# When routing makes its list: ahead of the scatters in attention 0, with weights asked for early and row copies one per step

## The chip, the cores and the metric

The kernel runs on one core of a Trainium2 chip. The metric is the device time of one execution in microseconds (us), given as a median over several runs. TensorE (PE) multiplies, VectorE (DVE) and ScalarE (ACT) work on tiles element by element, GpSimd (POOL) issues the indirect transfers, and SyncE (SP) issues the other transfers between the chip's memory (HBM) and the tiles.

## What is computed

The reference is two layers on x of 4 batches x 512 tokens x 256, all in fp32:

```python
x = x + L0_xattn(layernorm(x), ctx)      # 8 heads of 4
x = x + L0_ffn(layernorm(x))             # 8 experts, top 2, at most 640 tokens each
x = x + L1_xattn(layernorm(x), ctx)      # 16 heads of 16
x = x + L1_ffn(layernorm(x))             # 15 experts, top 3, and one shared expert
```

A token's expert in layer 0 is found from softmax logits, its place among that expert's tokens by counting in token order, and tokens beyond the capacity of 640 are dropped:

```python
probs = softmax(clip(xn @ Wr.T)); top_p, top_i = top_k(probs, 2)
rank  = position of the token among those that chose the same expert
buf[expert, rank] = xn[token]            # rank < 640
h = silu(buf @ Wg.T) * (buf @ Wu.T); y = h @ W3.T
out[token] += top_p * y[expert, rank]
```

## The kernel before

**Stages.** Attention 0, the experts of layer 0, attention 1, the experts of layer 1. The expert stages work on tiles of tokens of one expert. Which expert a tile has is known only at run time, so a list of tiles is made on the chip, and SyncE reads the numbers out of it with value loads (`fetch0`, L958) to address rows (`rows0`, from the table `slots` in HBM) and weights (`w12`, 2 MB, and `w3`, 1 MB, for one expert).

**Attention.** `attention` (L561) is written as a software pipeline over steps t, whose order on TensorE, VectorE and ScalarE is set by hand. A step does two score matmuls with their row maximum (`maximum`, L695 and L700), two transposed score matmuls with the exponential (`exponential`, L719 and L724), and in every second step the product with the values (`weigh`, L734). A planner places the rest (projections, transposes L708, outputs L791) into steps by cost and due time. LEAD is 11: the maxima run eleven steps ahead of the exponentials.

**Routing beside it.** When a batch's attention is done, a generator starts for it (`behind0` in layer 0, `behind1` in layer 1), which calls `route` (L242): layer norm, copies of the normed rows into the rows to be scattered by ScalarE (L250, four per batch), eight PE transposes (L267), logits (L279), top-k, the running counts `past` (L319 to 322), softmax weights (L326 to 331), the place of each token (L352 to 369), and then, per group of 128 tokens (four) and choice (two), a scatter of rows into `slots` by GpSimd (L380). The generator yields between steps: V and PEP (a piece of VectorE or TensorE work, which costs credit), ACT (a piece of ScalarE work), or LITTLE (a step that costs nothing). Each attention step advances each generator by up to two items (L903 to 921). `pause` says that a generator does no more in this step:

```python
pause = w[1] == LITTLE and not shared
```

`shared` is true in attention 0, so there it never pauses. `w[2]` is the batch. `early` means batches 0 and 1 in attention 0; `hurry` that all attention steps are over (t > 8 * N) or have not begun.

**The list.** `listing` (L404) makes the list from the counts: a matmul of `past` (L419), some fifteen small VectorE operations (L422 to 455), and a matmul that moves the list onto one partition (L460). Its PSUM tile, `bank`, is one buffer which routing's transposes, logits, ranks and lists and attention 0's projections share.

**Early pairs.** After batch 1's routing, three pairs of full tiles (AHEAD = 3) can already be worked on. So behind batch 1's `route`, `behind0` makes a first list (`ahead0`), fetches the rows of the three pairs and asks for the weights of the first two. The rows wait for all scatters issued so far (`ffn0.puts`). Once attention 0's steps are over, `some_pairs` (L1036) runs these pairs: `turn0` (transposes, L980), `hidden0` (L998, eight pieces of four matmuls of 128x256), and `output0` (L1016, with a result scatter by GpSimd at L1022). Between its pieces the routing of batches 2 and 3 goes on. Behind batch 3's `route` a second list (`list0`) is made, and `pipeline` (L468, called at L1121) runs the remaining tiles: it fetches a tile's rows and W12 two tiles ahead, its W3 one ahead. All these transfers are issued by SyncE, in program order, on one queue.

**Attention 1.** It has 768-element row copies (three choices), and `some_shared` (L1255) puts pieces of the shared expert into the steps once its own steps are over.

Of the kernel before, what the change touches and what calls it, by code (L numbers as in the profile page):

```python
# [23 lines left out]
B, S, D = 4, 512, 256  # L24
# [25 lines left out]
TILES0 = -(-CAP // P)  # L50
# [4 lines left out]
AHEAD = 3  # L55
FULL0 = [(i + 1) * PAIR - 1 for i in range(CAP // PAIR)]
MOST0 = T * K0 // P + E0 - 1
# [18 lines left out]
def decoder_kernel(ctx: ExitStack, tc: tile.TileContext, a: dict, out: bass.AP):  # L76
# [6 lines left out]
    def after(ins, earlier, reason):  # L83
        for e in earlier:
            tc.add_manual_dep(
                ins, e.name,
                mybir.DependencyInfo(mybir.DependencyClass.Sync, mybir.DependencyReason.DATA),
                reason=reason,
            )
# [53 lines left out]
    early = ExitStack()  # L143
# [39 lines left out]
    V, ACT, PEP, LITTLE = "VectorE", "ScalarE", "TensorE", "little"  # L183
# [55 lines left out]

            self.expert, self.slot, self.token, self.base = expert, slot, token, base  # L240

    def route(f, b, pool, bank):  # L242

        n, K, first = f.n, f.k, f is ffn0
        rows = []
# [74 lines left out]
        for k in range(TB):  # L320
            nc.vector.tensor_tensor(past[:, k + 1, :], past[:, k, :], picked[:, k, :], ALU.add)
        f.past[b] = past

        yield V
        total = small.tile([P, TB], F32, name="sm_sum", tag="sm_sum")
# [42 lines left out]
        at = small.tile([P, TB, K], F32, name="at", tag="at")  # L368
# [3 lines left out]


        for k in range(TB):
            for _ in range(2):
                yield LITTLE
            nc.gpsimd.tensor_copy(rows[k][:, :, D + 1], weight[:, k, :])  # L377
            nc.vector.tensor_copy(put[k], at[:, k, :])
            for j in range(K):
                ins = nc.gpsimd.indirect_dma_start(  # L380
                    out=f.rows,
                    out_offset=bass.IndirectOffsetOnAxis(ap=put[k][:, j : j + 1], axis=0),
                    in_=rows[k][:, j, :],
                    in_offset=None,
                ).ins
                after(ins, f.fills, "empty rows under the rows")
                group = "puts" if first else "puts1"
                tc.declare_no_dep(ins, group=group, reason="disjoint rows")
                tc.add_to_no_dep_group(group, ins)
                f.puts.append(ins)  # L390
# [170 lines left out]
    def attention(L, begin, behind, others=None):  # L561
# [6 lines left out]
        shared = L == 0  # L568
# [19 lines left out]
        for i in range(NV):  # L588
            v = ap.tile([P, TB, (H - 1) * VS + 32], F32, name=f"v{i}", bufs=1)
            nc.gpsimd.memset(v, 0.0 if shared else 1.0)  # L590
            if shared:
                r = v.rearrange("p t (h i) -> p (t h) i", i=64)
                for s in range(2):
                    at = s * (32 + VR) + HD
# [226 lines left out]
        for b in range(B):  # L821
            at = 8 * U * b - LEAD
            starts[at - (26 if shared else 34)] = [lambda b=b: normalize(b)]
            turned = [task(at - 14, at - 6, lambda b=b, c=c: turn(b, c)) for c in range(DC)]
            for g in range(G):
                at = 8 * (U * b + 2 * g) - LEAD
# [9 lines left out]
            at = 8 * U * b  # L836
# [39 lines left out]
        with tc.manual_schedule(engines={ENG.PE, ENG.DVE, ENG.Activation}):  # L876
            while t <= last or (others and (going or pieces)):

                for j2 in range(2):
                    n, i = divmod(t + LEAD, 8)  # L880
                    if 0 <= n < N:
                        maximum(units[n], i, j2)
                    n, i = divmod(t, 8)
                    if 0 <= n < N:
                        exponential(units[n], i, j2)
                n, i = divmod(t - 3, 8)
                if 0 <= n < N and i % 2 == 0:
                    u = units[n]
                    weigh(u, i // 2)
                    if i == 6 and (not shared or u[2] == 1):  # L890
                        rest[u] = divide(u)
                if t == 4 - LEAD:
                    warm(AF.Exp)
                free = t not in steps
                credit = min(credit + RATE[L], 2 * RATE[L])
                if not free:
                    steps[t][0]()
                    credit -= steps[t][1]
                for start in starts.get(t, []):
                    work = start()  # L900
                    going.append([work, next(work), None])

                for w in sorted(going, key=lambda w: w[2] is not None):  # L903

                    early = shared and w[2] in (0, 1)
                    hurry = t > 8 * N or t < -LEAD
                    for _ in range(MOST[w[2] if early else None] if shared else 2):
                        if w[1] == PEP:
                            if not free:
                                break  # L910
                            free = False
                        if w[1] in (V, PEP):
                            if credit < (DEBT if early else COST) and not hurry:
                                break
                            credit -= COST
                        pause = w[1] == LITTLE and not shared
                        w[1] = next(w[0], None)
                        if w[1] is None:
                            going.remove(w)
                        if w[1] is None or pause:  # L920
                            break
                if others and t == 8 * N + 2:
                    pieces = others(ps_sc, wp, ap)
                if pieces and next(pieces, V) is V:
                    pieces = None
                t += 1
# [15 lines left out]
    def rows_of(t):  # L942
        return [t[:, k] for k in range(TB)]

    ffn0 = Routing(
        E0, K0, wr0, slots, zeros, lambda b: rows_of(mr0.tile([P, TB, K0, ROW], F32, name="rows", tag="rows"))
    )
    ffn1 = Routing(E1, K1, gw, xs, zeros1, None)
    ahead0 = const.tile([1, 2 * AHEAD + 1], I32, name="ahead0")
    list0 = const.tile([1, 2 * MOST0 + 1], I32, name="list0")  # L950
# [7 lines left out]
    def fetch0(j):  # L958
        rows0[j] = mr.tile([P, 2, ROW], F32, name="rows0", tag="rows0")
        at, i, n = (ahead0, j, AHEAD) if j < AHEAD else (list0, j - AHEAD, MOST0)  # L960
        r = nc.sync.value_load(at[0:1, n + i : n + i + 1], min_val=0, max_val=E0 * TILES0)
        m = 2 if j < AHEAD else 1
        src = tiles0[bass.ds(r, m)].rearrange("s p d -> p s d")
        after(nc.sync.dma_start(rows0[j][:, :m], src).ins, ffn0.puts, "rows in the slots")
        experts0[j] = nc.sync.value_load(at[0:1, i : i + 1], min_val=0, max_val=E0 - 1)

    def fetch_w12(j):
        load_w0(w12, "w12", a["W12T"], j, experts0[j])

    def fetch_w3(j):  # L970
        load_w0(w3, "w3", a["W3T"], j, experts0[j])
# [99 lines left out]

    def behind0(b):
        ffn0.xT[b] = mr0.tile([P, DC, S], F32, name="xT0", tag="xT0", bufs=1)
        yield from route(ffn0, b, mr0, bank)
        if b == 1:
            yield from listing(ffn0, b, ml0, bank, TILES0, AHEAD, ffn0.full, ahead0, size=2)
            for j in range(AHEAD):
                fetch0(j)
                if j < 2:
                    fetch_w12(j)  # L1080
                    fetch_w3(j)
        if b == B - 1:
            yield from listing(
                ffn0, b, ml1, bank, TILES0, MOST0, ffn0.some, list0, ffn0.taken, AHEAD
            )

    ml1 = routing.enter_context(tc.tile_pool(name="m0m", bufs=1))
    attention(0, begin0, behind0, some_pairs)
# [2 lines left out]
    with ExitStack() as first:  # L1091
        ps_h = first.enter_context(tc.tile_pool(name="ps_h", bufs=2, space=PSUM))
        ps_y = first.enter_context(tc.tile_pool(name="ps_y", bufs=2, space=PSUM))
        ps_t = first.enter_context(tc.tile_pool(name="ps_t", bufs=2, space=PSUM))
        mw = first.enter_context(tc.tile_pool(name="m0w", bufs=2))
        w0p.append(first.enter_context(tc.tile_pool(name="w02", bufs=1)))
        new = dict(
            pt=lambda: ps_t.tile([P, DC, P], F32, name="prt", tag="prt"),
            pg=lambda: ps_h.tile([P, PAIR], F32, name="pg", tag="pg"),
            pu=lambda: ps_h.tile([P, PAIR], F32, name="pu", tag="pu"),  # L1100
            py=lambda: ps_y.tile([P, D], F32, name="py", tag="py"),
            rT=lambda: mw.tile([P, DC, P], F32, name="rT0", tag="rT0"),
            hT=lambda: mw.tile([P, NF // 2, PAIR], F32, name="hT", tag="hT"),
            sg=lambda: mw.tile([P, PAIR], F32, name="sg", tag="sg"),
            ysb=lambda: mw.tile([P, D], F32, name="ysb", tag="ysb", bufs=6),
            parts=NF // 2,
        )

        def fetch(j):
            fetch0(j)  # L1110
            fetch_w12(j)

        def hidden(j):
            for _ in hidden0(j, new):
                pass

        def output(j):
            for _ in output0(j, new):
                pass

        pipeline(  # L1121
            AHEAD, AHEAD + ALWAYS0, [AHEAD + h for h in THEN0],
            lambda: nc.values_load(list0[0:1, 2 * MOST0 :], min_val=0, max_val=MOST0) + AHEAD,
            fetch, lambda j: turn0(j, new), hidden, output, fetch_w3,
        )
# [378 lines left out]
```

## Time and profile before

| quantity | value |
|---|---|
| median of 3 runs | 1227.63 us (1227.49 to 1232.14) |
| the profiled execution | 1229.34 us |
| its span, first to last instruction | 1227.6 us |
| mean granted TensorE clock | 0.957 of full |
| TensorE busy | 1155.8 us (94%) |
| VectorE, ScalarE, GpSimd busy | 619.2, 460.0, 187.8 us |
| DMA | 204.74 MB, 167 GB/s over the span |
| attention 0's last value product (L734) ends | 202.4 us |
| early pairs, first hidden matmul to the last output | 213.7 to 295.2 us |

The page gives busy times per engine, the span in 40 slices (one digit each: tenths of the slice in which the engine was busy, or tenths of full clock that TensorE was granted), and groups of instructions by line. The timeline lists one engine's instructions with start and duration in us; the square brackets hold the idle time right before it and what ended it. A row of windows gives the busy time of each engine in a stretch (with the number of instructions), then the granted clock, the DMA engines' busy share, and the rate. PE busy in a stretch with a clock of 0.50 is busy at half speed.

### The profile page before, as it was taken

Reading aid. Unit: us, or ns where it says so; the run is one execution under the profiler, and the core shown is the slowest. Engines: PE = TensorE matmul, PEld = TensorE weight load, DVE = VectorE, ACT = ScalarE, POOL = GpSimd, SP = SyncE. Lnnn points to the kernel's source line nnn. Section 1 sums busy time; section 2 is a strip of 40 time slices with the busy share of each in tenths; the row PEclk is TensorE's granted clock in tenths of the full one; section 3 lists DMA queues with packets and bytes.
Section 4 is the critical chain, followed back from the end, with each engine's and each line's share of the span. In section 5 each row is a group of like instructions: output and inputs, shape, how many; then the busy total and the mean of one; then the engine's idle time right before and its main releaser. Section 6 shows DMA issues by size and latency. Waiting matters only on the chain.

```text
span 1227.6 us, 18270 instructions
## 1 busy us (share of the span) xinstructions
PE 1155.8 (94%) x6582; PEld 742.3 (60%) x6582; DVE 619.2 (50%) x1591; ACT 460.0 (37%) x877; POOL 187.8 (15%) x274
## 2 busy tenths in 40 slices
PE   6999995989999999999999999999999999999992
PEld 3334332778999999996333433433346558888862
DVE  7677763531112111115768778767625435444426
ACT  2455454422222222213365566565543102333320
POOL 2000202051000000002000000211212401333330
PEclk9899988999999999999799999999979989999996
DMA  8999205338778888853101000101100134777737
GB/s 319 406 404 403 80 1 210 125 112 315 286 271 321 332 308 308 318 218 105 35 1 36 1 1 1 40 14 40 40 18 35 52 109 137 222 233 222 223 119 252
DMA packets 64406, 204.74 MB, mean 167 GB/s; under 512 B 9502, under 2 KB 31922, under 8 KB 57392
## 3 DMA queue, kind: packets, MB, share of 16 engines
q1 hardware_dynamic: 56144, 182.93, 41.9%
q0 software_dynamic: 8160, 20.52, 4.5%
q8 instruction: 55, 0.90, 0.3%
q14 instruction: 47, 0.39, 0.1%
HBM read 138.57 MB, written 66.70 MB: 167 GB/s over the span
## 4 chain that ended last, share of the span: by engine, by line
PE 43%; DVE 5%; DMA 3%; issue 2%; ACT 1%; POOL 0%; SPq 0%; POOLq 0%; DVEq 0%; ACTq 0%
PE sc L695 9%; PE av L734 5%; PE pg L1292 4%; PE pv L1292 4%; PE shared L1173 3%; PE pyp L1346 3%; PE sct L719 2%; DVE negmax L700 2%; PE pp L672 2%; PE shared L1188 1%; DMA y<-ysb,rows 1%; DMA yr<-y 1%; PE po L791 1%; PE pa L644 1%; PE pa L672 1%
## 5 line engine op out<-in xcount | busy, mean ns | idle before, releaser
L700 DVE TENSOR_REDUCE negmax<-sc 128x1 f32<-128x512 f32 x384 | 245.1, 682 | 68.3 <-PE sct L719 61.7
L724 ACT ACTIVATE es<-sct 128x512 f32<-128x512 f32 x384 | 208.7, 595 | 167.7 <-PE sct L719 148.6
L695 PE MATMUL sc<-kT,qT 32*128 32x512 f32 x768 | 257.4, 663 | 7.4 <-DVE negmax L700 4.4
L719 PE MATMUL sct<-qa,kT 32*128 32x512 f32 x768 | 259.8, 661 | 1.7 <-DVE qa L710 1.7
L695 PEld LDWEIGHTS sc<-kT,qT 32*128 32x128 f32 x768 | 83.2, 189 | 106.5 <-DVE negmax L700 61.4
L1007 DVE TENSOR_TENSOR hT<-pu,sg 128x256 f32<-128x256 f32 x96 | 40.8, 425 | 136.6 <-PE pu L998 133.1
L734 PE MATMUL av<-es,v 128*32 128x512 f32 x768 | 109.0, 628 | 0.0
L998 PE MATMUL pg<-rT,w 128*128 128x128 f32 x768 | 101.8, 275 | 0.4 <-ACT ahead L1020 0.4
L998 PE MATMUL pu<-rT,w 128*128 128x128 f32 x768 | 101.4, 275 | 0.0
L719 PEld LDWEIGHTS sct<-qa,kT 32*128 32x128 f32 x768 | 80.3, 189 | 26.1 <-issue 15.5
L998 PEld LDWEIGHTS pg<-rT,w 128*128 128x128 f32 x768 | 93.6, 192 | 0.8 <-ACT ahead L1020 0.6
L998 PEld LDWEIGHTS pu<-rT,w 128*128 128x128 f32 x768 | 93.5, 192 | 0.0
L1016 PE MATMUL py<-w,hT 128*128 128x256 f32 x384 | 86.7, 379 | 0.0
L1353 POOL DMA_INDIRECT y<-ysb,rows x60 | 59.1, 985 | 154.0 <-ACT ysb L1351 142.7
L1016 PEld LDWEIGHTS py<-w,hT 128*128 128x128 f32 x384 | 71.2, 190 | 8.7
L1003 ACT ACTIVATE sg<-pg 128x256 f32<-128x256 f32 x96 | 36.9, 384 | 101.7 <-PE pg L998 100.7
L377 POOL COPY rows<-weight 128x2 f32<-128x2 f32 (+1 forms) x28 | 4.4, 210 | 458.0 <-DVE weight L340 262.4
L734 PEld LDWEIGHTS av<-es,v 128*32 128x32 f32 x768 | 16.2, 109 | 77.9 <-issue 70.8
L1292 PE MATMUL pg<-rTp,wp 128*128 128x256 f32 x240 | 61.8, 380 | 0.6 <-DVE rTp L1330 0.6
L1292 PE MATMUL pv<-rTp,wp 128*128 128x256 f32 x240 | 61.6, 379 | 0.0
L1022 POOL DMA_INDIRECT y<-ysb,rows x24 | 23.6, 984 | 237.0 <-ACT ysb L1020 234.5
L1159 DVE TENSOR_SCALAR aTp<-pv,wp 128x256 f32<-128x256 f32 x60 | 32.6, 544 | 51.5 <-PE pv L1292 50.4
(257 smaller groups left out, 1493.6 us busy)
## 6 DMA issues: line engine op xcount, KB each, us to landing
w<-in_W12T_dram SPq DMA_DIRECT2D x27, 2048.0 KB
xs<-empty SPq DMA_DIRECT2D x61, 516.0 KB
w<-in_W3T_dram SPq DMA_DIRECT2D x27, 1024.0 KB
wp<-in_w1p_dram SPq DMA_DIRECT2D x30, 515.0 KB
yr<-y SPq DMA_DIRECT2D x20, 512.0 KB
rows<-xs SPq DMA_DIRECT2D x30, 258.0 KB
wp<-in_fc2T_dram SPq DMA_DIRECT2D x30, 256.0 KB
slots<-empty SPq DMA_DIRECT2D x11, 516.0 KB
```

What stands on the lines that cost most here:

```text
L672: nc.tensor.matmul(pp, W["W" + n][:, c, g * P : (g + 1) * P], rhs[:, c, :], start=(c == 0), stop=(c == DC - 1),)
L695: nc.tensor.matmul(sc, q[u][32 * j : 32 * j + 32, qt * P : (qt + 1) * P], k[u][32 * j : 32 * j + 32, :], start=True, stop=True,)
L700: nc.vector.tensor_reduce(heads[:, qt, j, HELP[s] : HELP[s] + 1], sc, AX.X, ALU.max, negate=True)
L719: nc.tensor.matmul(sc, k[u][32 * j : 32 * j + 32, kt * P : (kt + 1) * P], qa[u][32 * j : 32 * j + 32, :], start=True, stop=True,)
L724: nc.scalar.activation(t, sc, AF.Exp, scale=p["scale"])
L734: nc.tensor.matmul(av[b, g][32 * j : 32 * j + 32, :], vs[b % NV][:, kt, h : h + 32], es[u, kt, j], start=(first and kt == 0), stop=(last a ...
L998: nc.tensor.matmul(ph[:, i * n : (i + 1) * n], w[:, c, col + i * P : col + (i + 1) * P], rT[:, c, :], start=(c == 0), stop=(c == DC - 1),)
L1003: nc.scalar.activation(sg, pg, AF.Silu)
L1007: nc.vector.tensor_tensor(h, pu, sg, ALU.mult)
L1016: nc.tensor.matmul(py, hT[f][:, i * P : (i + 1) * P], w[:, f, :], start=(f == 0), stop=(f == NF - 1))
L1292: nc.tensor.matmul(ph[:, :n], w1[:, c, col : col + P], rhs[:, c, :], start=(c == 0), stop=(c == DC - 1),)
L1353: ins = nc.gpsimd.indirect_dma_start(out=y1, out_offset=bass.IndirectOffsetOnAxis(ap=rows[:, i, D : D + 1].bitcast(I32), axis=0), in_=ysb[ ...
```

## The change

`route` gets a hook, `counted`, that it runs as soon as the counts are made, ahead of the weights, the places and the scatters. `behind0` uses it to make the lists there. For batch 1 it also reads the experts of the three pairs and asks for the weights of the first two at that point; the rows are still fetched behind the scatters. For this, `fetch0` is split: the expert's value load becomes `name0`. Batch 1's scatters get three LITTLE items per group of tokens where they had two. `pause` changes: in attention 0 the scatters of batches 0, 2 and 3 now take one LITTLE item per step, and ScalarE's row copies of batches 2 and 3 in attention 0 and of all batches in attention 1 go one per step until the steps are over.

```diff
-    def route(f, b, pool, bank):
+    def route(f, b, pool, bank, counted=lambda: iter(())):
...
         f.past[b] = past
+        yield from counted()
...
-            for _ in range(2):
+            for _ in range(3 if first and b == 1 else 2):
                 yield LITTLE
...
-                        pause = w[1] == LITTLE and not shared
+
+                        pause = (
+                            w[1] == LITTLE and not (shared and w[2] == 1)
+                            or w[1] == ACT and w[2] is not None and not hurry and not early
+                        )
...
         after(nc.sync.dma_start(rows0[j][:, :m], src).ins, ffn0.puts, "rows in the slots")
+
+    def name0(j):
+        at, i = (ahead0, j) if j < AHEAD else (list0, j - AHEAD)
         experts0[j] = nc.sync.value_load(at[0:1, i : i + 1], min_val=0, max_val=E0 - 1)
...
-        yield from route(ffn0, b, mr0, bank)
+
+        def counted():
+            if b == 1:
+                yield from listing(ffn0, b, ml0, bank, TILES0, AHEAD, ffn0.full, ahead0, size=2)
+                for j in range(AHEAD):
+                    name0(j)
+                for j in range(2):
+                    fetch_w12(j)
+                    fetch_w3(j)
+            if b == B - 1:
+                yield from listing(
+                    ffn0, b, ml1, bank, TILES0, MOST0, ffn0.some, list0, ffn0.taken, AHEAD
+                )
+
+        yield from route(ffn0, b, mr0, bank, counted)
         if b == 1:
-            yield from listing(ffn0, b, ml0, bank, TILES0, AHEAD, ffn0.full, ahead0, size=2)
             for j in range(AHEAD):
                 fetch0(j)
-                if j < 2:
-                    fetch_w12(j)
-                    fetch_w3(j)
-        if b == B - 1:
-            yield from listing(
-                ffn0, b, ml1, bank, TILES0, MOST0, ffn0.some, list0, ffn0.taken, AHEAD
-            )
...
         def fetch(j):
             fetch0(j)
+            name0(j)
             fetch_w12(j)
```

## The prediction, made before the change was run

> **What bounds the kernel now.** I read the page first: which engine carries the span and where its clock falls.
>
> ```profile
> PE 1155.8 (94%) x6582; PEld 742.3 (60%) x6582; DVE 619.2 (50%) x1591; ACT 460.0 (37%) x877; POOL 187.8 (15%) x274
> ...
> PEclk9899988999999999999799999999979989999996
> ```
>
> TensorE is busy 94% of the span, so 1227.6 - 1155.8 = 72 us is all that filling idle time could bring, plus what lost clock costs (mean granted clock 0.957). A routing edit is worth only the TensorE stops it removes and the half-clock stretches behind them. Slice 7 (184 to 215 us) and slice 30 (890 to 921 us) are the two weak ones that touch routing. So next the windows of slice 7:
>
> ```profile
> core 0: us, PE busy (x) PEld busy (x) DVE busy (x) ACT busy (x) POOL busy (x), PEclk, DMA share, GB/s
> ...
> 194.00:200.00 6.00, 2.78 (x29) 0.79 (x22) 4.27 (x25) 2.83 (x6) 0.55 (x4) 1.00 0.03 9
> 200.00:204.00 4.00, 2.86 (x16) 0.96 (x12) 1.16 (x8) 3.81 (x7) 0.00 (x0) 1.00 0.70 189
> 204.00:208.00 4.00, 0.62 (x6) 0.38 (x4) 1.10 (x3) 1.46 (x3) 0.00 (x0) 0.81 0.99 412
> 208.00:212.00 4.00, 0.00 (x0) 0.00 (x0) 0.00 (x0) 0.00 (x0) 0.00 (x0) 0.50 1.04 427
> ```
>
> The DMA engines idle until 200 us, then run full while TensorE stands still. TensorE's timeline (start, duration, instruction, idle before with its releaser) names the waits; its last two rows are the same wait for batch 3's list:
>
> ```profile
> 197.73 0.35 PE L460 MATMUL bank<-ident,list_both 128*1 128x3 f32 x4 [3.22 <-DVE list_both L453]
> ...
> 212.76 1.12 PE L980 MATMUL ahead<-ident,rows 128*128 128x128 f32 x4 [8.13 <-DMA rows<-slots]
> 213.67 3.39 PE L998 MATMUL ahead<-ahead,w 128*128 128x256 f32 x8
> ...
> 274.05 0.40 PE L460 MATMUL bank<-ident,list_both 128*1 128x39 f32 x4 [3.67 <-DVE list_both L453]
> 274.38 7.13 PE L998 MATMUL ahead<-ahead,w 128*128 128x256 f32 x24
> ```
>
> The queues of SyncE (SP) and GpSimd (POOL) say when things were asked for: batch 1's last scatter starts at 192.27, weights are asked for from 201.03.
>
> ```profile
> 201.03 0.35 SPq L153 DMA_DIRECT2D w<-in_W12T_dram  x1
> ...
> 192.27 0.97 POOL L380 DMA_INDIRECT slots<-rows,put  x1 [0.30 <-DMA slots<-rows,put]
> ```
>
> Last, slice 30 and just ahead of it, attention 1, batch 2's routing: TensorE's transposes wait for ScalarE's row copies, and then the clock is half for 20 us although TensorE is full.
>
> ```profile
> 884.22 0.33 PE L267 MATMUL bank<-ident,rows 128*128 128x128 f32 x1 [0.58 <-ACT rows L250]
> 886.11 0.48 PE L267 MATMUL bank<-ident,rows 128*128 128x128 f32 x1 [1.56 <-ACT rows L250]
> ```
>
> ```profile
> 884.00:886.00 2.00, 0.33 (x1) 0.14 (x1) 0.00 (x0) 2.00 (x4) 0.00 (x0) 0.92 0.00 0
> 886.00:892.00 6.00, 5.89 (x19) 2.11 (x21) 0.69 (x1) 1.60 (x4) 0.00 (x0) 0.50 0.00 0
> 892.00:900.00 8.00, 8.00 (x28) 3.06 (x24) 0.69 (x1) 2.30 (x5) 0.00 (x0) 0.50 0.00 0
> 900.00:906.00 6.00, 6.00 (x28) 2.80 (x29) 2.53 (x18) 2.20 (x6) 0.00 (x0) 0.50 0.00 0
> ```
>
> **1. Batch 1's list, scatters, weights, rows.** In the changed program order the count matmul of the list stands right behind the av at 178.46, when the counts are made (DVE 178.23 to 179.0). The list's VectorE chain took 3.2 us (194.88 to 198.1); TensorE has two sct pairs, ptm and an av meanwhile, 1.13 + 0.66 + 1.13 + 1.06 = 4.0 us, so the 3.22 us stop shrinks to about 0.3 and the list is there at about 184.3. Three value loads of expert numbers on SP (1.1 to 1.5 us each, by the gaps of SP's issues) put the first weight issue at 188, 13 us earlier. Two pairs are 6.29 MB; at 410 GB/s of the windows 15.3 us, so they end at 204 to 207.5.
>
> The scatters pay: the place matmul (L352) is now behind the next av, and VectorE's place chain (1.15 us) and one more yield follow, so the first put comes at about 192.9 where it was 182.5. POOL needs 0.8 us to start and 1.275 us per scatter: 193.9 to 204.1, 11 us later. The bytes land 1.6 to 2 us past POOL, now with the weights on the same DMA engines. SP's row fetches stand behind four weight issues and wait for all scatters: asked at 206 to 208, landed (two fetches, 1.1 us apart, and a flight of about 2.3 us, estimated from rows(3), issued at 275.73 on an empty queue, whose bytes move until about 278) at 209.4 to 211.3. First hidden matmul at 210.3 to 212.2, taken 211.2, for 213.67: **-2.5** (-3.4 to -1.5). What is late next is the scatters' landing, no longer the weights. TensorE still stands about 6 us and the half clock behind it (3.39 us for 8 matmuls) stays.
>
> Against this edit speaks the Trainium skill ("DMA: Bandwidth & Descriptors", Queues, rings and completion order): a DMA engine takes turns between queues packet by packet. With five queues busy, the 1.06 MB of scatters would get a fifth of 410 = 82 GB/s, 12.9 us, and the last byte would land at about 208, rows at 211.3 (the late end). By the trace's nearest row (POOL 264.92 to 268.75, scatters beside a 1 MB load at 216 GB/s) pitch and landing don't stretch, rows at 209.4. I take the middle; both leave a gain.
>
> **2. The three early pairs.** Before, TensorE stops 1.75 us (240.87, L352 behind xT), 3.67 us (274.05), and loses some 1.7 us of half clock behind the latter (window 274 to 278: 0.59): 7.1 us. After, the list's matmuls lie between hidden pieces of 1.0 us. Four stops remain by walking the order: L353 behind `past`, about 1.0; L267 behind the bank, 1.3 less what fills it, 1.0; L419 behind `past`, 1.3; L460 behind the list, 1.0: sum 4.3. None reaches the 3.67 us that lost the clock here. **-2.8** (-4 to -1).
>
> **3. Start of the later tiles.** Let X be the start of the last 14 us of outputs (281.35 before; first turn 295.16). Batch 3's first put now comes some 6 us ahead of X, so its eight scatters end at X + 4 and land at X + 6; they ended 12 us ahead of X. Behind them on SP wait rows(3), w12(3), rows(4). rows(3) goes at X + 6, its 2 MB of W12 at X + 7.1 and at 378 GB/s plus flight lands at X + 14; TensorE's outputs end at X + 14. **+0.3** (0 to 2), with no slack left. POOL's result scatters now stand between batch 3's; nobody reads them before attention 1.
>
> **4. Batches 0, 2, 3: one scatter step at a time.** Same instructions; batch 0's end at about 158 for 150.2, hidden by POOL's idle time (15% busy). Its cover is 30 us of attention. The clock was 0.5 at 148 to 152 and 156 to 162 with no long idle ahead; that can move either way, 0, -4 to +4.
>
> **5. One ScalarE row copy per step.** In attention 1, batch 2, TensorE waits 0.58 + 1.56 = **2.14 us** for copies of 1.03 us each, queued in front of the transposes. After, the four transposes come four steps later, behind 2 sct, av, 2 sct, ptm, 2 sct, av. ScalarE then has es 1.08 + one copy 1.03 = 2.1 us per step against TensorE's step of about 2.1: no new queue, but nothing to spare (0 to +1). Batch 1's 0.5 us of the same kind goes too: **-0.5**. The routing of batch 2 ends four steps later; batch 3's part, the shared expert and the layer's end keep their order, and TensorE-bound work passes the gain on.
>
> The clock: 20.4 us at 0.50 (886 to 906.5) did work that takes half that (sct x4 2.08 us for 1.06), so 10.2 us hang on whether the drop goes with its stop. The skill ("TensorE: Matmul & The Clock Gate", Part 1: The HAM clock gate) says about 3.4 us of idle halve the clock and 3.4 us of work restore it, in a free-running window. By the rule 2.14 us of idle would hardly drop it, and the loss would be 3.4 / 2 = 1.7 us. By the row it drops and stays 20 us. The measurement decides its size; that the stop caused it is an inference: 640 to 880 us ran at 1.00 without such a stop, the drop falls in the stop's own 2 us, but 3.22 us at 194.5 did not drop it. I take -7.5: 10.2 less 2.7 in which VectorE or ScalarE would bound at full clock. Ends: 0 and -10.2. With the stop **-9.6**, less 0.5 for ScalarE's tightness: **-9.1**.
>
> **Sum**: -2.5 - 2.8 + 0.3 - 0.5 - 9.1 = -14.6. The profiled execution took 1229.34 (1227.6 span and 1.7 around it), so 1214.7; it stood 1.7 above the median, so the median goes to 1227.63 - 14.6 = **1213**. I forecast 1214, the rounding kept to the side of less.
>
> **Rivals.**
> (a) The half clock of 886 stays, or returns elsewhere in attention 1: for it, the 0.5 stretches at 148 to 162 without a long stop; against, its place. Then 7.5 less gain: about 1221.
> (b) Only stops move: scatters land late (-0.5 at most in 1), the four stops of the pairs add up to the old 7, +2 at the tiles' start, and the clock drop stays, leaving the 2.6 of copies: 1227. This is also the case that the change doesn't do what it says: weights asked early, rows not earlier.
> (c) Slower: batch 3's scatters. Point 3 has no slack: every us by which their landing passes X + 6 holds rows(3), then W12, then TensorE. At X + 18 (if the puts wait for steps held by the bank) that is 12 us of stop, and a stop over 3.67 us loses the clock, at worst 20 us at half as at 886, 10 us. With (a)'s -7 this makes 1227.6 - 7 + 22 = 1242. It decides from X + 13 on: 7 us of stop and 6 of half clock make 1234.
>
> **Chances.** The forecast 0.50, (a) 0.25, (b) 0.14, (c) 0.11. What a measurement tells from no change is about 0.5%, 6.1 us: 1221.5 to 1233.8. Faster: 0.50 and most of (a), 0.66; same: the rest of (a) and (b), 0.23; slower: (c), 0.11. The range reaches from all of the clock's 10.2 and the good ends (1207) to (b)'s end (1228).
>
> **What would show it.** Right: weights issued at about 188, L460's stop under 1 us, first hidden matmul near 211, rows(3) issued 6 us behind the outputs' start, the L267 waits of attention 1 gone and clock 1.00 near 890. Wrong: a stop over 3 us at the tiles' first turn (c), clock 0.50 for 20 us in attention 1 (a), or rows asked for past 209 (b).

## The result, and the profile after

The changed kernel took 1211.31 us (median of 4 runs, 1206.49 to 1216.69) beside 1228.95 us for the kernel before (4 runs): ratio 0.9848, 95% interval 0.9813 to 0.9883. The forecast was 1214. That figure must be read with a second one. The experiments below ran later, on three chips on which the kernel before takes 1210.6 to 1211.2 us; there the changed kernel, run again, gave 0.9968 (0.9954 to 0.9982), 22 runs beside 47. So the change is a gain in both comparisons, but a fifth of the size where before is not slow to start with. On which chip the first comparison ran is not on record. Much of this section and the next is about why.

The profiled execution after took 1215.69 us, with a span of 1214.0 us. Its page:

```profile
PE 1149.4 (95%) x6582; PEld 738.3 (61%) x6582; DVE 620.4 (51%) x1591; ACT 459.5 (38%) x877; POOL 186.5 (15%) x274
...
PEclk7899998999999999999699999999989989999996
```

TensorE is still the bound; slice 30 is a little better (8 for 7), the first slice is worse (7 for 9). The windows of the stop at the early pairs (start and end, length, busy time and count of PE, PEld, DVE, ACT, POOL, then granted clock, DMA share, GB/s):

```profile
194.00:200.00 6.00, 5.86 (x36) 1.53 (x32) 1.26 (x9) 5.44 (x11) 4.49 (x5) 0.98 1.00 423
200.00:204.00 4.00, 1.16 (x5) 0.34 (x3) 0.00 (x0) 0.93 (x3) 1.93 (x2) 1.00 0.99 380
204.00:208.00 4.00, 1.59 (x5) 0.90 (x5) 1.08 (x2) 1.15 (x2) 0.14 (x2) 0.57 0.24 94
208.00:212.00 4.00, 1.09 (x4) 0.71 (x4) 0.38 (x3) 0.00 (x0) 0.41 (x4) 0.50 0.56 139
```

The DMA engines now work while attention still runs, as the change meant, and have little left to do from 204 us. Yet TensorE stands as long as before. Its timeline shows for what; then the queues of SyncE and GpSimd:

```profile
182.51 0.36 PE L461 MATMUL bank<-ident,list_both 128*1 128x3 f32 x4 [0.29 <-DVE list_both L454]
...
212.46 1.12 PE L988 MATMUL ahead<-ident,rows 128*128 128x128 f32 x4 [0.50 <-DMA rows<-slots]
213.37 2.59 PE L1006 MATMUL ahead<-ahead,w 128*128 128x256 f32 x8
...
258.13 0.40 PE L461 MATMUL bank<-ident,list_both 128*1 128x39 f32 x4
```

```profile
185.22 0.36 SPq L153 DMA_DIRECT2D w<-in_W12T_dram  x1
...
208.10 2.71 SPq L969 DMA_DIRECT2D rows<-slots  x3
```

```profile
201.28 0.96 POOL L381 DMA_INDIRECT slots<-rows,put  x1 [0.30 <-issue]
207.86 0.55 POOL L261 COPY rows<-token 128x2 f32<-128x2 f32 x4 [5.61 <-DMA slots<-rows,put]
```

The list's stop is gone (0.29 us) and the weights are asked for at 185 instead of 201. But the last scatter starts at 201.28 (192.27 before), GpSimd's next instruction waits 5.61 us behind it for the scatters' landing, SyncE asks for the rows at 208.10, and the first hidden matmul comes at 213.37, where it was 213.67. For the last 3 us of that wait the DMA engines are almost idle (41 GB/s and less from 205 us on): the landing is set by a few late packets.

To see where the time went, I line up the value products (L734 before, L735 after, 96 groups in the same order in both) and subtract the starts. The second column of numbers does this for two later traces of the same two kernels on the experiments' chips (before_again and changed_again below).

| at | gained so far, first pair (us) | second pair (us) |
|---|---|---|
| first value product of attention 0 | -4.2 | +2.6 |
| value product at 164 us of before | +2.1 | +2.7 |
| last of attention 0 | +1.9 | +2.6 |
| first hidden matmul of the early pairs | +0.3 | -0.8 |
| first hidden matmul of the later tiles | +4.1 | +0.7 |
| first value product of attention 1 | +2.7 | -0.4 |
| behind the copies of batch 0 (746 us of before) | +4.9 | +1.9 |
| behind the copies of batch 1 (831 us) | +7.3 | +4.3 |
| last of attention 1 | +14.8 | +7.1 |
| end of the span | +13.6 | +8.3 |

Three things stand out. Up to the first row the instructions are the same, and the pairs already differ by 4.2 and 2.6 us in opposite directions. The clock differs there too: in the first 47 us it is half for 10 us in before and for 24 us in each of the other three traces. Next, the early pairs start no earlier: from the value product at 164 us to their first hidden matmul the changed kernel loses 2.1 - 0.3 = 1.8 us in the first pair and 2.7 + 0.8 = 3.5 us in the second. And the whole stage the change is named for, lists and early weights, brings little: between 164 us and the first value product of attention 1 it is 2.7 - 2.1 = +0.6 us in the first pair and -0.4 - 2.7 = -3.1 us in the second, while attention 1 gives 12.1 and 7.5 us.

### The profile page after: what moved, and what is told of

It is laid out like the page before. It is cut to its first block, busy times and chain, and to the rows that moved or that the text cites. A ratio compares the mean times of both kernels' runs of the same rounds, so it can differ in the third digit from the quotient of the medians.

```text
span 1214.0 us, 18265 instructions
## 1 busy us (share of the span) xinstructions
PE 1149.4 (95%) x6582; PEld 738.3 (61%) x6582; DVE 620.4 (51%) x1591; ACT 459.5 (38%) x877; POOL 186.5 (15%) x274
## 4 chain that ended last, share of the span: by engine, by line
PE 44%; DMA 5%; DVE 4%; issue 1%; ACT 0%; POOL 0%; SPq 0%; DVEq 0%; POOLq 0%
PE sc L696 10%; PE av L735 5%; PE shared L1188 4%; PE pg L1307 3%; PE pv L1307 3%; PE pyp L1361 3%; PE sct L720 3%; DMA y<-ysb,rows 2%; DMA yr<-y 2%; PE pp L673 2%; DVE negmax L701 2%; PE shared L1203 1%; PE po L792 1%; PE pa L645 1%; PE pa L673 1%
## 5 line engine op out<-in xcount | busy, mean ns | idle before, releaser
L725 ACT ACTIVATE es<-sct 128x512 f32<-128x512 f32 x384 | 208.5, 596 | 155.2 <-PE sct L720 143.6
L720 PE MATMUL sct<-qa,kT 32*128 32x512 f32 x768 | 254.3, 660 | 1.7 <-DVE qa L711 1.7
L735 PE MATMUL av<-es,v 128*32 128x512 f32 x768 | 107.2, 619 | 0.1
L735 PEld LDWEIGHTS av<-es,v 128*32 128x32 f32 x768 | 16.0, 109 | 76.7 <-issue 70.6
```

Of the source, the lines that this page charges most:

```text
L720: nc.tensor.matmul(sc, k[u][32 * j : 32 * j + 32, kt * P : (kt + 1) * P], qa[u][32 * j : 32 * j + 32, :], start=True, stop=True,)
L725: nc.scalar.activation(t, sc, AF.Exp, scale=p["scale"])
L735: nc.tensor.matmul(av[b, g][32 * j : 32 * j + 32, :], vs[b % NV][:, kt, h : h + 32], es[u, kt, j], start=(first and kt == 0), stop=(last a ...
```

## Experiments

On all of these the ratio is to the kernel before on the same chip.

**Copies or lists?** The change has two clauses of pause and the new order. Four kernels take them apart.

copies_undone is the changed kernel with

```diff
-                            or w[1] == ACT and w[2] is not None and not hurry and not early
```

> The changed kernel with one clause of the pause taken back: ScalarE's row copies again go up to two per step; lists, early weights and spread scatters stay. Theory COPIES (in attention 1 the unpaced copies hold up exponentials, and the two score matmuls of a step no longer overlap, which the busy time of TensorE hides): the time rises by 7 to 12 us over the changed kernel, to 1218 to 1223. Theory LISTS (the early list and weights bring the gain, the copies are noise of the clock): it stays at 1209 to 1213.

Measured: 1214.04 us, ratio 1.0028 (1.0012 to 1.0043): the lists, early weights and spread scatters together cost 0.3%, some 3.4 us.

copies_alone is the kernel before with that clause added to its pause.

> The kernel before with that clause alone: one row copy per step for batches 2 and 3 of attention 0 and all of attention 1. COPIES: 7 to 12 us below before, 1217 to 1222, with the value products of batches 0 and 1 in attention 1 some 5 us earlier. LISTS: 1227 to 1231.

Measured: 1203.47 us, ratio 0.9937 (0.9918 to 0.9956): -7.6 us.

lists_alone is the changed kernel with the pause of before:

```diff
-                        pause = (
-                            w[1] == LITTLE and not (shared and w[2] == 1)
-                            or w[1] == ACT and w[2] is not None and not hurry and not early
-                        )
+                        pause = w[1] == LITTLE and not shared
```

> The changed kernel with the whole pause of before: list ahead of the scatters, early weights and three LITTLE steps for batch 1, but neither scatters nor copies are spread. COPIES: 2 to 5 us below before (the stops on the two lists go, the rows come no earlier), 1224 to 1227. LISTS: 10 us or more below before, under 1218.

Measured: 1214.76 us, ratio 1.0045 (1.0026 to 1.0064). Not even the 2 to 5 us that I still gave it: the lists and early weights are a loss of about 5 us (3 to 8 by the interval, which overlaps that of copies_undone).

scatters_alone is the kernel before with the first half of the new pause, `w[1] == LITTLE and not (shared and w[2] == 1)`.

> The kernel before with only the scatters of batches 0, 2 and 3 in attention 0 one step at a time. If the half clock at 148 to 162 us in before comes from batch 0's scatters lying together: 3 to 6 us below before, 1223 to 1226, with the clock at 1.00 there. If that dip was chance: within 1.5 us of before, and the dip seen or not seen independently of the edit.

Measured: 1211.99 us, ratio 1.0000 (0.9985 to 1.0016). Spreading the scatters does nothing that shows, within 2 us. The clock was 1.00 at 148 to 162 us in this trace, but so it was in before_again without the edit, and at 148 to 152 it was 0.61 in copies_batch01: chance.

changed_again is the changed kernel itself.

> The changed kernel once more, beside runs of before on the chip of these experiments, where before takes some 1210.6 us and not 1228. If the parts add up (copies -7, lists and early weights with later scatters +3.5): 1206 to 1208, 0.3% below before. If the 1.5% of the first comparison holds on every chip: about 1192.

Measured: 1207.76 us, ratio 0.9968: the parts add up (-7.6 + 3.4 = -4.2; measured -3.9).

**Which copies, and by what?** The prediction put nearly all of the gain in batch 2 and its clock.

```diff
-                        pause = w[1] == LITTLE and not shared
+                        pause = (
+                            w[1] == LITTLE and not shared
+                            or w[1] == ACT and not shared and w[2] == 2 and not hurry
+                        )
```

> The kernel before with one row copy per step for batch 2 of attention 1 alone. If the half clock behind 886 us hung on the stop at the transposes, as the prediction took it: 7 us or more below before. If the half clock comes anyway and only the stop goes: 2 to 3 us below before, with a stretch at 0.50 still seen near 880 to 900 us.

Measured: 1207.19 us, ratio 0.9969 (0.9954 to 0.9985), -3.8 us, and clock 0.66 and 0.77 in the windows 888 to 894 and 894 to 900.

copies_batch01 has `w[2] in (0, 1)` in that place.

> The kernel before with one row copy per step for batches 0 and 1 of attention 1 alone. If unpaced copies cost overlap of the two score matmuls without idle time showing: 3 to 5 us below before. If what shows as idle is all there is (0.6 us for batch 1, none for batch 0): within 1 us of before.

Measured: ratio 0.9977 (0.9961 to 0.9993), -2.8 us (0.8 to 4.7 by the interval); the two medians, 1210.16 and 1210.69, lie closer together than that. The size lies between the two expectations, but 0.6 us of visible idle time is not all: in both pairs of traces above, the stretches of these two batches' copies give 2.2 and 2.4 to 2.5 us. ScalarE's timeline of before, batch 0, shows what else:

```profile
708.93 1.94 ACT L250 ACTIVATE rows<-x,shift,r 128x768 f32<-128x768 f32 x2
710.76 1.07 ACT L724 ACTIVATE es<-sct 128x512 f32<-128x512 f32 x2
```

and TensorE's in the same place:

```profile
710.24 0.69 PE L695 MATMUL sc<-kT,qT 32*128 32x512 f32 x1
...
710.79 0.59 PE L695 MATMUL sc<-kT,qT 32*128 32x512 f32 x1
711.41 1.12 PE L719 MATMUL sct<-qa,kT 32*128 32x512 f32 x2
712.46 1.07 PE L734 MATMUL av<-es,v 128*32 128x512 f32 x8
```

Two copies in a row hold the exponentials back by 1.94 us, so the step's second two sct matmuls (they free their PSUM tiles through those exponentials) start behind the last sc, not beside it, and run alone for 1.12 us. In the changed kernel the copies come singly, and sc and sct start within 0.3 us of each other:

```profile
708.14 1.04 ACT L250 ACTIVATE rows<-x,shift,r 128x768 f32<-128x768 f32 x1
```

```profile
707.58 0.69 PE L696 MATMUL sc<-kT,qT 32*128 32x512 f32 x1
...
708.13 0.59 PE L696 MATMUL sc<-kT,qT 32*128 32x512 f32 x1
708.36 0.59 PE L720 MATMUL sct<-qa,kT 32*128 32x512 f32 x1
708.88 1.07 PE L735 MATMUL av<-es,v 128*32 128x512 f32 x8
```

From the step's first sc to the value product it is 712.46 - 710.24 = 2.22 us before and 708.88 - 707.58 = 1.30 us after. TensorE counts as busy throughout (6.00 of 6.00 in the window 712 to 718 of before); what is lost is the overlap of two matmuls that use 32 rows each.

**The half clock of batch 2.** TensorE's timeline after, where before stopped for 2.14 us at the transposes:

```profile
880.78 0.66 PE L267 MATMUL bank<-ident,rows 128*128 128x128 f32 x4
...
885.07 1.96 PE L279 MATMUL bank<-gateT,xT 128*128 128x15 f32 x16
886.96 1.88 PE L720 MATMUL sct<-qa,kT 32*128 32x512 f32 x4
```

and the windows there:

```profile
880.00:884.00 4.00, 4.00 (x24) 1.44 (x16) 0.69 (x1) 3.03 (x7) 0.00 (x0) 1.00 0.00 0
884.00:886.00 2.00, 2.00 (x19) 1.09 (x17) 0.00 (x0) 1.82 (x4) 0.00 (x0) 1.00 0.00 0
886.00:892.00 6.00, 6.00 (x26) 2.64 (x29) 2.63 (x19) 1.36 (x4) 0.00 (x0) 0.60 0.01 3
```

The stop is gone, TensorE is full, and the clock halves all the same, for some 10 us. Across the six traces in which batch 2's copies are not paced the same stop stands in each (0.58 + 1.56 us, to 0.01 us), and the stretch at half clock that follows is about 20 us (before), 27 (copies_batch01 and scatters_alone), 7 (before_again), 3 (copies_undone and lists_alone). With paced copies it is about 10 us (after and copies_alone) and 7 us (changed_again, copies_batch2 and scatters_first). So the drop does not hang on the stop. Its length varies between executions; that the three long ones are all with the stop may be chance, and these runs don't settle it. In before_again and changed_again the half clock is 7 us in both, and there the table's gain from batch 1's copies to the end of attention 1 is 7.1 - 4.3 = 2.8 us: little more than the stop of 2.1.

**Why are the rows late?** scatters_first keeps the changed kernel, but puts the list's steps between batch 1's scatters and the rows ahead of most weights:

```diff
-        yield from counted()
+        beside, listed_ = first and b == 1, counted()
+        if not beside:
+            yield from listed_
...
-            for _ in range(3 if first and b == 1 else 2):
-                yield LITTLE
+            for _ in range(2):
+                yield next(listed_, LITTLE) if beside else LITTLE
...
                 for j in range(AHEAD):
                     name0(j)
-                for j in range(2):
-                    fetch_w12(j)
-                    fetch_w3(j)
+                fetch_w12(0)
...
             for j in range(AHEAD):
                 fetch0(j)
+            fetch_w3(0)
+            fetch_w12(1)
+            fetch_w3(1)
```

> The changed kernel with batch 1's order turned: the list's steps lie between the scatters (in place of their LITTLE steps), so the scatters start as early as before; on SyncE first W12 of pair 0, then the rows of the three pairs, then W3 of pair 0 and pair 1's weights. If the changed kernel's rows are late because the scatters come 10 us later and land among the weights: rows asked for at about 198 instead of 208, first hidden matmul near 204 instead of 213, 7 to 9 us below the changed kernel. If the stop has another cause (the weights themselves, ScalarE held up while the DMA engines are full): no more than 2 us below it.

Measured: 1198.04 us, ratio 0.9902 (0.9879 to 0.9924), 0.7% (8 us) below the changed kernel by the ratios. SyncE and TensorE:

```profile
186.19 0.36 SPq L153 DMA_DIRECT2D w<-in_W12T_dram  x1
196.46 2.74 SPq L974 DMA_DIRECT2D rows<-slots  x3
```

```profile
199.57 0.63 PE L993 MATMUL ahead<-ident,rows 128*128 128x128 f32 x4 [1.25 <-DMA rows<-slots]
200.91 1.11 PE L993 MATMUL ahead<-ident,rows 128*128 128x128 f32 x4 [0.72 <-DMA rows<-slots]
201.82 3.04 PE L1011 MATMUL ahead<-ahead,w 128*128 128x256 f32 x8
```

The rows are asked for 12 us earlier, the waits for them are 2 us, and the first hidden matmul is at 201.82. Some 3 us of that lie ahead of the routing: from the value product near 164 us to the first hidden matmul it is 43.4 us, where the changed kernel takes 51.5 (changed_again) and the kernel before 48.0 (before_again). Is it the early weight or the place of the rows? first_weights_late moves that one `fetch_w12(0)` behind the rows.

> scatters_first with all four weight transfers asked for behind the rows, at about 200 us, instead of W12 of pair 0 at 186. If asking early for weights is worth what the change took it for: 2 MB at 410 GB/s and the flight, so the first hidden matmul comes at about 206 to 207 instead of 202, with more half clock, and the time is 4 to 6 us above scatters_first. If only the order of scatters and rows matters: within 1.5 us of scatters_first.

Measured: 1200.23 us, ratio 0.9912 (0.9890 to 0.9933). TensorE waits once for W12:

```profile
203.46 3.64 PE L1011 MATMUL ahead<-ahead,w 128*128 128x256 f32 x8 [3.03 <-DMA w<-in_W12T_dram]
```

That is 3 us of stop at most, and the interval overlaps that of scatters_first. So nearly all of the gain over the changed kernel comes from rows that can go out early: scatters that start as early as in before, and rows ahead of the weights on the queue. These two were not tested apart. In the kernel before, the second pair's rows stood on SyncE's queue behind 3 MB of the first pair's weights, and the second `turn0` needs them ahead of the first hidden matmul:

```profile
201.56 0.33 SPq L153 DMA_DIRECT2D w<-in_W3T_dram  x1
202.67 0.38 SPq L964 DMA_DIRECT2D rows<-slots  x1
```

By the DMA packets of this trace, the first pair's W12 moves from 202.1 to 208.5, its W3 from 207.6 to 211.3, and the second pair's rows, asked for at 202.67, only from 210.0 to 212.3. In the changed kernel the rows stood behind the scatters. Against copies_alone (0.9937), which has no early list at all, scatters_first gains some 4 us, so that much is what the early list and the rows bring in this order; the two intervals touch.

**Batch 3.** Two variants of scatters_first: its list put back behind `route` (first_list3_behind), and its scatters as dense as before, `w[2] in (1, 3)` in the pause (first_scat3_together).

> scatters_first with batch 3's list put back behind its scatters, as in before. If the early list of batch 3 is worth its removed stop (3.67 us in before, and the half clock behind it): 2 to 4 us above scatters_first, 1200 to 1202. If it only moves the wait to the first tiles' rows (a stop of 2.2 us there in scatters_first): within 1.5 us of it.

> scatters_first with batch 3's scatters (and not its list) as dense as in before. If they hold up the rows of the first later tile: rows(3) asked for 2 to 4 us earlier, the 2.2 us stop at the tiles' start and the half clock behind it gone, 1 to 4 us below scatters_first. If POOL's own pace or the puts' place in the order decides: no difference.

Measured: 1197.16 us, ratio 0.9892 (0.9865 to 0.9920), and 1199.21 us, 0.9890 (0.9869 to 0.9912). Neither differs from scatters_first, by intervals of some 3 us to either side. The early list of batch 3 is worth nothing that can be measured.

**The kernel before once more**, for its trace.

> The kernel before once more, for its trace on the kind of chip where it takes 1210 us. If the first profile of before was long by half-clock stretches that come and go (28 to 40, 148 to 162, 886 to 906 us): several of them are shorter or gone here with the same instructions, and the 8 us wait for the early pairs' rows is still there. If before is long by its own order: the same stretches at the same places.

Measured: 1216.95 us in the one run, span 1215.0. The half clock at 148 to 162 is gone, that behind the transposes is 7 us, and the early pairs' wait is there. And the two stops that the prediction counted on are small:

```profile
196.87 0.36 PE L460 MATMUL bank<-ident,list_both 128*1 128x3 f32 x4 [0.90 <-DVE list_both L453]
...
211.61 1.12 PE L980 MATMUL ahead<-ident,rows 128*128 128x128 f32 x4 [7.84 <-DMA rows<-slots]
...
272.51 0.40 PE L460 MATMUL bank<-ident,list_both 128*1 128x39 f32 x4 [0.64 <-DVE list_both L453]
```

0.90 and 0.64 us where the first trace had 3.22 and 3.67, with the same instructions. The list's first step (L422) shows what was late. It needs the count matmul L419, which ends at 192.44 in the first trace and at 193.91 here:

```profile
194.88 0.17 DVE L422 TENSOR_TENSOR list_more<-bank,full 128x16 f32<-128x16 f32 x1 [2.72 <-PE av L734]
194.91 2.06 ACT L724 ACTIVATE es<-sct 128x512 f32<-128x512 f32 x4 [1.78 <-PE av L734]
```

```profile
194.01 0.17 DVE L422 TENSOR_TENSOR list_more<-bank,full 128x16 f32<-128x16 f32 x1 [0.67 <-PE bank L419]
```

In the first trace (upper lines) VectorE starts 2.4 us behind that matmul's shown end, here 0.1 us, and ScalarE, which waits for TensorE as well, goes on within 0.03 us of VectorE. So it was TensorE's results that came late, and VectorE was not slow. At the second list it is alike: L422 starts 3.2 us behind the end of its count matmul in the first trace, 0.3 us here. TensorE's ends are modelled in the profile, so part of those 3.22 and 3.67 us may have been work and not idle time. Why TensorE's results came late in that execution stays open.

## Why the prediction came out right, and where it did not

**The total** was right in the comparison that it was made for, and the steps behind it were partly wrong. Luck had a large part in it. Step 1 was forecast as a gain and was a loss, attention 1 gave more than forecast, in part because the half clock of before was long in that trace, and the stretch up to 164 us, with its changing half clock, gave 2.1 us that no step had forecast. With the same instructions on the later chips the gain is 3.9 us, not 14.6.

**Step 1, batch 1 (-2.5).** Wrong, in sign too. The weights went out at 185 (188 was said) and the list's stop shrank to 0.29, as said; the first scatter started at 192.38 (192.9). The failed term is the scatters' landing, put at 1.6 to 2 us past GpSimd, 3.9 at the late end: it was 5.6 us with the weights on the same DMA engines, so the rows went out at 208.10, just past the late end of 206 to 208. The rows themselves then took 4.4 us, from 208.10 to the second pair's transposes at 212.46, where two fetches 1.1 us apart and a flight of 2.3 make 3.4. The Trainium skill's rule ("DMA: Bandwidth & Descriptors", Queues, rings and completion order) that engines take turns between queues pointed this way, and I took the middle between it and the row. But the fifth that I made of it has no ground: I counted five busy queues, and the traces have two that move data here, one with SyncE's transfers and one with GpSimd's. By its packets the scatters' bytes moved for 10.4 us, not 12.9, and the first of them 4.4 us behind the first scatter's start (1.5 in before); why so late is not shown. At the first hidden matmul the table has +0.3, but it had +2.1 at 164 us, so the step lost 1.8 us where a gain of 2.5 was forecast, and 3.5 in the second pair. This is what rival (b) named, weights asked early and rows not earlier. The prediction also took the 8 us wait to lie with scatters and weights, and did not see that the rows of the second pair stood behind the first pair's weights. scatters_first and first_weights_late show that rows asked for ahead of the weights remove most of the wait.

**Step 2, early pairs (-2.8).** Right in the first pair of traces (from +0.3 to +4.1, of which 1.4 came back by the start of attention 1). The four stops that I walked to 4.3 us were 0.72 + 0.97 + 1.63 = 3.3 and none at batch 3's list. But the 3.67 us they replace (and the 3.22 of step 1) did not come again: 0.64 and 0.90 in before_again. One profiled execution was taken for the kernel. On the later chips steps 1 to 3 together are a loss: 3.4 us by copies_undone, 5 by lists_alone.

**Step 3, the later tiles (+0.3).** Right, at the high end of its range. rows(3) was issued at 281.81, 5.5 us behind the outputs' start at 276.27 (6 said); TensorE waits 1.05 and 0.75 us, within the 0 to 2. Rival (c) did not come.

**Step 4, scatters (0).** Right: ratio 1.0000 for them alone.

**Step 5, row copies (-9.6 with the clock).** The place was right, the mechanism half. The stop went and ScalarE's pace of one copy per step fits, as walked. The clock's -7.5 was mis-sized: the drop came back 5 us behind the transposes with no stop, and batch 2's pacing is worth 3.8 us, of which the stop is 2.1. What I put at 0.5, batches 0 and 1, is 2.8: overlap of matmuls lost behind a busy TensorE, which idle time doesn't show. In the first pair of traces the stretch was long before (20 us) and shorter after (10), so the whole of attention 1 gave 12.1 us, where 9.6 was forecast. Rival (a), half clock that stays or returns, was thus true in part: its 0.5% of gain is nearer to the 0.3% of the second comparison than the forecast is.

## What to carry to other kernels

In these traces transfers on one queue moved in the order in which they were issued (rows asked for at 202.67 moved from 210.0, behind 3 MB): ask first for the small one that the next instruction needs, then for the megabytes, and keep the stores it depends on ahead of both. Where two matmuls run beside each other, look at the time per step and not at the engine's idle time, since a late partner makes a step longer (2.22 us for 1.30 here) while TensorE stays busy. Take two traces of the kernel before you price a stop or a half-clock stretch from one.

## What the runs showed of the hardware

A stretch of half clock came at full TensorE with no stop ahead of it (887 us after), and behind one and the same stop of 2.14 us it lasted between 3 and 27 us in six traces. The scatters' landing went from 1.6 us at most (before) and 1.9 us (before_again) behind the last one, with no other transfers beside them, to 5.6 us where weight loads had filled the DMA engines at 380 to 423 GB/s until 204 us (after), while GpSimd's own pace stayed at 1.27 us per scatter. VectorE got TensorE's count matmul 2.4 us behind its shown end in one execution of a kernel (before) and 0.1 us behind it in another (before_again).
